# Gated experts with residual: how closing pairs are added up, and the queue of the first weights

## The chip, the cores and the metric

The kernel runs on one core of a Trainium2 chip. The metric is the device time of one execution in microseconds. TensorE (PE) multiplies matrices, VectorE (DVE) and ScalarE (ACT) work element by element and can read and write the PSUM banks that PE fills, GpSimd (POOL) works element by element in SBUF only, and SyncE (SP) issues most transfers. Each engine takes its instructions in the order of its own list, and waits on semaphores for the others.

## The reference

A residual block with 8 gated experts and one shared expert, all in float32, for x of 8 examples, 512 positions and 256 features; F is 1024:

```python
g = einsum('bsd,edf->ebsf', h, Wg)
u = einsum('bsd,edf->ebsf', h, Wu)
expert_outs = einsum('ebsf,efd->ebsd', silu(g) * u, Wd)
expert_output = einsum('be,ebsd->bsd', gating_probs, expert_outs)
shared = einsum('bsf,fd->bsd', silu(h @ Sg) * (h @ Su), Sd)
out = x + (1.0 - sg) * expert_output + sg * shared
```

Every example goes through all experts; the gates (`fside_Bx8_0`, `condB_sharedgateprob`) are 8 numbers and one number for each example.

## The kernel before

**Units.** The batch is cut into two halves of 4 examples, each expert's F into two groups of 4 blocks of 128. One half, expert and group is a unit: 2 x 9 x 2 = 36 units, in that order. In a unit stand 4 weight blocks against 4 examples, 16 products of a block with an example, for Wg, Wu and Wd. The kernel makes them with fewer multiplications than the plain way: for each of the 6 pairs (i, j) in `PAIRS`, products of sums and differences of the operands are shared between (i, j) and (j, i). The numbers `CI` of the four indices give each pair its d = CI[i] - CI[j]; d is 1 for pairs 0, 1 and 4, and 2, 2 and 3 for pairs 2, 3 and 5. GpSimd makes the sums and differences of weights (`make_at`, `w_difference`, `w_sums`, `make_ad`, `d_forms`).

**Two parts.** `gate_up` makes g, u and h of a unit: the hub steps P, Q and R (L466, L489, L511 are matmuls of it, L482 and L484 DVE differences of their results, L472, L499 and L506 ScalarE copies), then for each pair more matmuls (L521), DVE additions (L516, L526), silu on ScalarE (L452) and h on DVE (L457). `h_sums` makes X, the difference of a pair's two h (DVE, L537), and GpSimd adds the h into sums of rows and columns, called rows and cols (`add_sum`, L548).

`down` multiplies by Wd. It keeps running sums in SBUF over all 18 units of a half: accb and accB for each example (the two halves of the 256 features), and accS and accV for each pair. `pair(p)` has three steps: r, a matmul into a bank A (L607), added by DVE into accB (L578); S (or s), whose bank is first filled by a ScalarE copy of accS (L590) before PE multiplies onto it (L591), or s, which starts an empty bank (L607); and a second matmul onto A (L630), which DVE then adds into accV. After pairs come q and p for each example: q (L607) is a matmul on cols, and p (the bank b, L590 and L591) on rows. `put` is what adds a bank into a sum: L578 adds, L580 subtracts, L582 multiplies by a factor and adds.

**Closing.** In the last unit of a half, a pair's V is done and goes into accb of both its examples, +V/d into i and -V/d into j (`closes`). In half 0 all six pairs close in one unit; in half 1, pairs 3, 4 and 5 close one unit earlier, in unit 34, since the last unit makes only pairs 0, 1 and 2 this way. That makes 12 closings, between 1183 and 1231 us, 2349 and 2371 us, and 2393 and 2412 us. A closing is three DVE operations at the end of `pair`: A += accV in the bank (L634), then accb of i and of j from the bank (L578 and L580 where d is 1, L582 twice where it isn't). The two banks that `down` uses, po0 and po1, take turns. A is held (`held`) from the pair's first step to its last, so the other bank serves S; after the closing A's bank is the one that the next product takes (`po_next`).

**Order.** The orders of PE and GpSimd are written out by hand: the strings `HUB`, `BLOCK`, `ORDER`, `FIRST` and `LAST` say when a step of `gate_up` (G) and when one of `down` (D) follows. The down part of a unit starts at G step 22 (`TAKE`) of that unit, and goes on into the next. ScalarE's order is by hand in unit 0 alone. Everywhere else DVE and ScalarE are put in order by a scheduler.

**The start.** `load_gates` issues two transfers on ScalarE's queue, gt (L109) and sgt (L113), of the gates spread over 128 partitions. Everything else comes over SP's queue: the four examples' rows xin (two transfers each, L156) and the four blocks' Wg and Wu (w, two transfers each, L364; 128 partitions x 2 rows of 512 bytes). The first block's Wg stands between the two halves of the first rows, its Wu after them. `first_products` turns the first example and multiplies it with Wg (L202); after it `make_coef` on GpSimd makes the gates' factors (L118 to L121) and `make_at` the sums of the weights (L383 to L387). Transfers use eight semaphores in turn, those of both queues together, and an issue waits until the transfer that used its semaphore before has landed.

Of the kernel before, what the change touches and what calls it, by code (L numbers as in the profile page):

```python
# [11 lines left out]
ALU = mybir.AluOpType  # L12
# [4 lines left out]
def kernel(  # L17
# [37 lines left out]
    nc = tc.nc  # L55
# [24 lines left out]
    hpool = ctx.enter_context(tc.tile_pool(name="h", bufs=11))  # L80
# [16 lines left out]
    gp = nc.gpsimd  # L97
    ve = nc.vector

    def weights(e):  # L100
        return (Wg[e], Wu[e], Wd[e]) if e < E else (Sg, Su, Sd)
# [6 lines left out]
    def load_gates():  # L108
        nc.scalar.dma_start(  # L109
            gt.rearrange("p b e -> p (b e)"),  # L110
            gates.rearrange("b e -> (b e)").partition_broadcast(P),
        )
        nc.scalar.dma_start(sgt, shared_gate.partition_broadcast(P))  # L113
# [20 lines left out]
    def new_po(name, turns=False):  # L134

        k = po_next[0]
        if held[k]:
            k = 1 - k
        if not turns:
            po_next[0] = 1 - k  # L140
        return ps_o.tile([P, S], F32, tag=f"po{k}", name=name), k
# [2 lines left out]
        for t, block in enumerate(blocks):  # L144
            nc.tensor.transpose(bank[:, ts(t, P)], block, ident)

    def load_rows(pool, tag, b, between=None):
        rows = []
        for c in range(2):
            if pool is not iopool:  # L150
                t = pool.tile([P, 2, D], F32, tag=tag, name=f"xin{b}_{c}")
            elif c == 0:
                both = pool.tile([P, NT, D], F32, tag=tag, name=f"xin{b}")
            if pool is iopool:
                t = both[:, 2 * c : 2 * c + 2]
            nc.sync.dma_start(  # L156
                t, x[b].rearrange("(p t) d -> p t d", t=NT)[:, 2 * c : 2 * c + 2, :]
            )
            rows.append(t)
            if between and c == 0:  # L160
                between()
        return rows


# [161 lines left out]
    def touch_banks():  # L326

        banks = [
            pool.tile([P, S], F32, tag=tag, name=f"touch{tag}{k}")
            for pool, tag, n in ((ps_g, "g0", 3), (ps_g, "g1", 3), (ps_o, "po0", 1), (ps_o, "po1", 1))  # L330
            for k in range(n)
        ]
        zero = zpool.tile([P, 2 * S], mybir.dt.bfloat16, tag="z", name="zero")[:, :S]
        ve.memset(zero, 0.0)
        warm = const.tile([P, 1], F32, name="warm")
        nc.scalar.activation(warm, ident[:, 0:1], AF.Silu)
        for bank in banks:
            nc.tensor.matmul(bank, zero[:, 0:P], zero, start=True, stop=True)
# [4 lines left out]
    units = []  # L343
    for h in range(NH):
        for e in range(NE):
            for g in range(GRP):
                u = Unit()
# [8 lines left out]
                u.ad, u.Ud, u.Wd = {}, {}, {}  # L356
                units.append(u)

    def load_w(u, i, ms=(0, 1)):
        if i not in u.raw:  # L360
            u.raw[i] = wpool.tile([P, 2, 2, P], F32, tag="w", name=f"w{u.name}_{i}")
        t = u.raw[i]
        for m in ms:
            nc.sync.dma_start(  # L364
                t[:, m],
                weights(u.e)[m][:, ts(NI * u.g + i, P)].rearrange(
                    "(k p) f -> p k f", p=P
                ),
            )
# [180 lines left out]
    def flush_sums(u, which, n):  # L550
        while any(w == which and k == n for w, k, _ in u.sums):
            add_sum(u)

    def starred(u, p):

        return u.n + 1 < len(units) or p < STARRED

    def closes(u, p):

        return u.closes and starred(u, p) or u.n + 2 == len(units) and p >= STARRED  # L560

    def down(u, acc):

        def tile_of(key):
            acc[key] = apool.tile(
                [P, S], F32, tag=f"acc{key[0]}{key[1]}", name=f"acc{key[0]}{key[1]}_{u.h}"
            )
            return acc[key]

        def put(key, bank, s):  # L570

            if key not in acc:
                if s == 1.0:
                    nc.scalar.copy(tile_of(key), bank)
                else:
                    nc.scalar.mul(tile_of(key), bank, s)
            elif s == 1.0:
                ve.tensor_add(acc[key], bank, acc[key])  # L578
            elif s == -1.0:
                ve.tensor_sub(acc[key], acc[key], bank)  # L580
            else:
                ve.scalar_tensor_tensor(acc[key], bank, s, acc[key], ALU.mult, ALU.add)  # L582

        def seeded(key, w, b):

            po, k = new_po(f"{key[0]}{key[1]}_{u.name}")
            full = key in acc and not turned[k]
            turned[k] = False
            if full:
                nc.scalar.copy(po, acc[key])  # L590
            nc.tensor.matmul(  # L591
                po, w, b, start=not full, stop=True, skip_group_check=full
            )
            return po, full

        def carried(key, w, b):
            po, full = seeded(key, w, b)
            if full:
                nc.scalar.copy(acc[key], po)
            else:  # L600
                put(key, po, 1.0)
            return po if full else acc[key]

        def single(key, w, b):
            po, k = new_po(f"{key[0]}{key[1]}_{u.name}")
            turned[k] = False
            nc.tensor.matmul(po, w, b, start=True, stop=True)  # L607
            return po, k

        def pair(p):  # L610
            i, j = PAIRS[p]
            d = CI[i] - CI[j]
            A, k = single(("r", p), u.Wd[p][i], u.h_[i, j])
            put(("B", j), A, 1.0)
            held[k] = True
            yield
            args = u.Wd[p][j], u.h_[j, i]
            if p in OWN and not closes(u, p):
                carried(("S", p), *args)
            else:  # L620
                if p in OWN:
                    o, full = seeded(("S", p), *args)
                    if not full:
                        ve.tensor_add(o, o, acc["S", p])
                else:
                    o, _ = single(("s", p), *args)
                put(("B", i), o, -1.0)
                put(("V", p), o, -1.0)
            yield
            nc.tensor.matmul(  # L630
                A, u.Ud[p], u.X[p], start=False, stop=True, skip_group_check=True
            )
            if closes(u, p):
                ve.tensor_add(A, A, acc["V", p])  # L634
                put(("b", i), A, 1.0 / d)
                put(("b", j), A, -1.0 / d)
            else:
                put(("V", p), A, 1.0)
            held[k] = False
            po_next[0] = 1 - k  # L640
            yield

        if u.n + 1 < len(units):
            order = (0, 1, 2, 3, 4, "p0", "q0", 5, "q1", "p1", "q2", "p2", "q3", "p3")
        else:
            order = (0, 1, 2, "q1", "q2", "p1", "q0", "p2", "q3", "p0", "p3")
        done = {}
        for what in order:
            if isinstance(what, int):
                yield from pair(what)  # L650
                continue
            i = int(what[1])
            if what[0] == "p":
                flush_sums(u, "rows", i)
                done[what] = carried(("b", i), u.raw_d[:, i, 0:P], u.rows[i])
            else:
                flush_sums(u, "cols", i)
                po, _ = single(("q", i), u.ad[i], u.cols[i])
                put(("B", i), po, 1.0)
                done[what] = po  # L660
            if u.closes and f"p{i}" in done and f"q{i}" in done:
                if CI[i] != 0.0:
                    put(("B", i), done[f"p{i}"], -CI[i])
                for r in (0, 1):
                    ends[u.h, i, r] = acc["bB"[r], i]
            yield
# [67 lines left out]
    def gate_up(u, nxt):  # L734
# [100 lines left out]
    by_hand.enter_context(  # L835
        tc.manual_schedule(engines=HAND | {mybir.EngineType.Activation})
    )
    load_gates()
    touch_banks()
    loaded = []  # L840
    for i in range(NI):
        if i == 0:
            loaded.append(load_rows(hpool, "h", i, lambda: load_w(units[0], 0, (0,))))
            load_w(units[0], i, (1,))
            continue
        loaded.append(load_rows(hpool, "h", i))
        load_w(units[0], i)
    turning = turn_x(0, loaded)
    first_products(units[0], loaded[0])
    for m in range(2):  # L850
# [5 lines left out]
    behind, acc, ahead = iter(()), {}, prepare(1)  # L856
    for u in units:
# [6 lines left out]
        for what in FIRST if u.n == 0 else LAST if nxt is None else ORDER:  # L864
            if what == "G":
                if nG == TAKE:
                    for _ in behind:
                        pass
                    if u.opens:
                        acc = {}  # L870
# [24 lines left out]
            elif what == "X":  # L895
                i, j, pools = TAILS.pop(0)
# [60 lines left out]
```

## Time and profile before

| | |
|---|---|
| three runs | 2445.86, 2445.99, 2448.1 us; median 2445.99 |
| the profiled execution's span, first to last instruction | 2444.9 us |
| lies around the span (median less span) | 1.1 us |
| PE's first and last matmul | 1.19, ends at 2441.08 us |
| DVE: X (L537), two SBUF inputs | 213 times, mean 978 ns |
| DVE: L634 of the closings | 12 times, mean 696 ns |
| GpSimd: sums of rows, further ones (L548) | 282 times, mean 1321 ns |
| GpSimd: sums of columns, further ones (L548) | 282 times, mean 1280 ns |
| GpSimd: first sums of rows and of columns (L548) | 144 times each, means 1385 and 1294 ns |
| median landing of gt and sgt after their issue | 4.0 and 5.7 us |

The profiled execution's own time isn't given apart from its span; the three runs stand for it. A float32 matmul with 512 columns appears as two passes (x2), and its start is 0.43 us after the pass before it where PE isn't kept waiting; so PE is read by the distance of starts, not by the duration of one (593 ns), since passes overlap. In a line of the timeline stand the start and the duration in us, the engine, the line of the kernel, the operation, what it writes and reads, and, in brackets, how long the engine was idle before it and what ended that. A line of the timeline with x2 or more is several instructions in a row. SPq and ACTq are the issues of transfers.

### The profile page before, as it was taken

The numbers are of one execution on the slowest core, as the hardware profiler recorded it, in microseconds if no ns is written. First come the engines' busy times: TensorE is split into PE (matmuls) and PEld (weight loads), VectorE is DVE, ScalarE is ACT, GpSimd is POOL, SyncE is SP. The second block draws the span as 40 slices with busy tenths as digits, with TensorE's granted clock in tenths as the row PEclk, the third lists the DMA queues.
The fourth block names the chain that finished last, engine by engine and source line by source line (L and its number), as shares of the span: only waits on it lengthen the run. The fifth ranks groups of instructions, "written<-read, shape, count | busy, mean of one in ns | idle before, by whom it ended". The sixth has DMA issues, their size and how long they took to land.

```text
span 2444.9 us, 22752 instructions
## 1 busy us (share of the span) xinstructions
PE 2431.5 (99%) x5722; PEld 1079.6 (44%) x5722; DVE 1937.4 (79%) x2889; ACT 1247.2 (51%) x2308; POOL 2095.8 (86%) x2335
## 2 busy tenths in 40 slices
PE   9999999999999999999999999999999999999998
PEld 4444444444444444444444444444444444444444
DVE  7777878777777777787997777777877777777787
ACT  4555554554555555545455555555455455555543
POOL 7988888898988989898888888888888888888883
PEclk9999999999999999999999999999999999999999
DMA  4333333343333333344353222322333333232322
GB/s 160 99 104 112 101 113 114 103 134 100 128 108 97 106 111 95 106 131 126 112 138 119 92 84 90 96 84 88 100 103 103 104 95 95 84 95 89 95 91 82
DMA packets 219793, 255.82 MB, mean 105 GB/s; under 512 B 63632, under 2 KB 156048, under 8 KB 219664
## 3 DMA queue, kind: packets, MB, share of 16 engines
q1 hardware_dynamic: 219376, 254.34, 34.3%
q8 instruction: 48, 0.79, 0.1%
q14 instruction: 81, 0.66, 0.1%
q10 hardware_dynamic: 288, 0.04, 0.0%
HBM read 238.59 MB, written 15.73 MB: 104 GB/s over the span
## 4 chain that ended last, share of the span: by engine, by line
PE 96%; DVE 1%; POOL 1%; DMA 0%; issue 0%; ACT 0%; SPq 0%; DVEq 0%; ACTq 0%; POOLq 0%
PE c L521 30%; PE c L511 15%; PE c L489 10%; PE c L466 10%; PE r L607 7%; PE r L630 7%; PE S L591 5%; PE b L591 5%; PE q L607 5%; PE s L607 2%; PE tail L715 0%; DVE h L457 0%; POOL wd L437 0%; DMA sgt<-ondB_sharedgateprob_dram 0%; DVE accb L582 0%
## 5 line engine op out<-in xcount | busy, mean ns | idle before, releaser
L521 PE MATMUL c<-b,wb 128*128 128x512 f32 x1728 | 847.5, 592 | 0.0
L452 ACT ACTIVATE sg<-c 128x512 f32<-128x512 f32 x576 | 343.8, 597 | 587.2 <-DVE c L526 343.6
L457 DVE SCALAR_TENSOR_TENSOR h<-sg,coef,c 128x512 f32<-128x512 f32 x576 | 427.8, 743 | 235.1 <-PE c L521 132.4
L521 PEld LDWEIGHTS c<-b,wb 128*128 128x128 f32 x1728 | 327.9, 190 | 412.4 <-issue 389.8
L511 PE MATMUL c<-v,u 128*128 128x512 f32 x864 | 441.6, 593 | 1.2 <-ACT c L506 1.2
L548 POOL TENSOR_TENSOR rows<-rows,h 128x512 f32<-128x512 f32 x282 | 372.4, 1321 | 0.0
L548 POOL TENSOR_TENSOR cols<-cols,h 128x512 f32<-128x512 f32 x282 | 361.0, 1280 | 0.0
L516 DVE TENSOR_TENSOR c<-D,c 128x512 f32<-128x512 f32 x432 | 298.9, 692 | 77.8 <-ACT sg L452 57.9
L526 DVE TENSOR_TENSOR c<-c,D 128x512 f32<-128x512 f32 x432 | 298.6, 691 | 18.7 <-PE c L521 18.5
L466 PE MATMUL c<-x,w 128*128 128x512 f32 x572 | 274.5, 592 | 0.0
L404 POOL TENSOR_TENSOR wb<-u,wb 128x256 f32<-128x256 f32 x108 | 79.0, 732 | 222.4 <-ACT wb L402 222.4
L511 PEld LDWEIGHTS c<-v,u 128*128 128x128 f32 x864 | 163.4, 190 | 209.2 <-issue 167.4
L607 PE MATMUL r<-h,wd 128*128 128x512 f32 x426 | 217.5, 592 | 0.0
L630 PE MATMUL r<-X,ud 128*128 128x512 f32 x426 | 217.5, 592 | 0.0
L537 DVE TENSOR_TENSOR X<-h,h 128x512 f32<-128x512 f32 x213 | 208.4, 978 | 6.9
L489 PE MATMUL c<-x,at 128*128 128x512 f32 x432 | 209.6, 593 | 2.4 <-DVE P L482 2.2
L499 ACT COPY D<-c 128x512 f32<-128x512 f32 x284 | 165.9, 584 | 86.8 <-DVE h L457 86.8
L548 POOL TENSOR_TENSOR rows<-h,h 128x512 f32<-128x512 f32 x144 | 199.5, 1385 | 0.0
L548 POOL TENSOR_TENSOR cols<-h,h 128x512 f32<-128x512 f32 x144 | 186.4, 1294 | 0.0
L472 ACT COPY P<-c 128x512 f32<-128x512 f32 x216 | 126.6, 587 | 107.0 <-PE c L466 102.5
L466 PEld LDWEIGHTS c<-x,w 128*128 128x128 f32 x572 | 108.5, 190 | 135.8 <-issue 111.4
L590 ACT COPY S<-accS 128x512 f32<-128x512 f32 x135 | 79.6, 590 | 152.7 <-DVE accV L578 144.9
(110 smaller groups left out, 3478.4 us busy)
## 6 DMA issues: line engine op xcount, KB each, us to landing
b<-xs SPq DMA_DIRECT2D x210, 512.0 KB, 3.6
v<-xs SPq DMA_DIRECT2D x210, 256.0 KB, 2.6
w<-in_L_cond_Wg_dram SPq DMA_DIRECT2D x128, 128.0 KB, 3.4
w<-in_L_cond_Wu_dram SPq DMA_DIRECT2D x128, 128.0 KB, 3.5
wd<-in_L_cond_Wd_dram SPq DMA_DIRECT2D x32, 512.0 KB, 5.0
f<-xd SPq DMA_DIRECT2D x12, 512.0 KB, 3.3
xs<-f SPq DMA_DIRECT2D x18, 256.0 KB, 3.0
xin<-in_x_dram SPq DMA_DIRECT2D x16, 256.0 KB, 4.0
```

What stands on the lines that cost most here:

```text
L452: nc.scalar.activation(s, bank, AF.Silu)
L457: ve.scalar_tensor_tensor(t, u.sg[i, j], coef[:, u.e, b : b + 1], bank, ALU.mult, ALU.mult)
L466: nc.tensor.matmul(bank, u.raw[i][:, m, 0], xhub[u.h, i][:, 0], start=True, stop=True)
L489: nc.tensor.matmul(bank, u.at[i][:, m], xhub[u.h, i][:, 1], start=False, stop=True, skip_group_check=True,)
L511: nc.tensor.matmul(bank, u.U[p][:, m], u.V[p], start=False, stop=True, skip_group_check=True)
L516: ve.tensor_sub(other, u.Ds[j, m], bank)
L521: nc.tensor.matmul(bank, u.W[p][:, r, m], u.VB[p][:, r], start=False, stop=True, skip_group_check=True,)
L526: ve.tensor_add(bank, bank, u.Ds[j, m])
L548: gp.tensor_tensor(sums[n], u.h_[n, n] if first else sums[n], u.h_[at], ALU.add)
L591: nc.tensor.matmul(po, w, b, start=not full, stop=True, skip_group_check=full)
L607: nc.tensor.matmul(po, w, b, start=True, stop=True)
L630: nc.tensor.matmul(A, u.Ud[p], u.X[p], start=False, stop=True, skip_group_check=True)
```

## The change

- In `down`, a closing pair's bank is added into V in SBUF by the one DVE operation that every other pair has too (`put(("V", p), A, 1.0)`), and the bank is let go. The pair is put on a list, `late`.
- `close_late`, called in the first step of the next pair (after its accB addition) or before the next p or q, makes the two results from V: on GpSimd, by two additions in SBUF, where d is 1; on DVE, by `put` with the factor 1/d, where it isn't. So 12 of the 24 results are made by GpSimd (6 in half 0, 6 in half 1).
- The first block's Wg and Wu are issued on ScalarE's queue, ahead of gt and sgt, and no longer among the first rows on SP's. The helper's argument for that (`between`, `ms`) goes.
- PE's order of instructions stays. In the built program DVE has 12 instructions fewer and GpSimd 12 more. In half 0 the two results of pair 5 stand on DVE behind the six operations of the next unit's P steps (L482); the ones before it stand near the place of the closing. SP's issues wait in turn for w0 Wg, w0 Wu, gt and sgt where they waited for gt, the first rows and sgt; block 2's Wu is the one that waits for sgt.

```diff
--- before.py
+++ after.py
@@ -144,7 +144,7 @@
         for t, block in enumerate(blocks):
             nc.tensor.transpose(bank[:, ts(t, P)], block, ident)
 
-    def load_rows(pool, tag, b, between=None):
+    def load_rows(pool, tag, b):
         rows = []
         for c in range(2):
             if pool is not iopool:
@@ -157,8 +157,6 @@
                 t, x[b].rearrange("(p t) d -> p t d", t=NT)[:, 2 * c : 2 * c + 2, :]
             )
             rows.append(t)
-            if between and c == 0:
-                between()
         return rows
 
 
@@ -356,12 +354,12 @@
                 u.ad, u.Ud, u.Wd = {}, {}, {}
                 units.append(u)
 
-    def load_w(u, i, ms=(0, 1)):
+    def load_w(u, i, queue=nc.sync):
         if i not in u.raw:
             u.raw[i] = wpool.tile([P, 2, 2, P], F32, tag="w", name=f"w{u.name}_{i}")
         t = u.raw[i]
-        for m in ms:
-            nc.sync.dma_start(
+        for m in range(2):
+            queue.dma_start(
                 t[:, m],
                 weights(u.e)[m][:, ts(NI * u.g + i, P)].rearrange(
                     "(k p) f -> p k f", p=P
@@ -607,12 +605,27 @@
             nc.tensor.matmul(po, w, b, start=True, stop=True)
             return po, k
 
+        late = []
+
+        def close_late():
+
+            while late:
+                p, i, j, d = late.pop(0)
+                V = acc["V", p]
+                if d == 1.0:
+                    gp.tensor_tensor(acc["b", i], acc["b", i], V, ALU.add)
+                    gp.tensor_tensor(acc["b", j], acc["b", j], V, ALU.subtract)
+                else:
+                    put(("b", i), V, 1.0 / d)
+                    put(("b", j), V, -1.0 / d)
+
         def pair(p):
             i, j = PAIRS[p]
             d = CI[i] - CI[j]
             A, k = single(("r", p), u.Wd[p][i], u.h_[i, j])
             put(("B", j), A, 1.0)
             held[k] = True
+            close_late()
             yield
             args = u.Wd[p][j], u.h_[j, i]
             if p in OWN and not closes(u, p):
@@ -630,12 +643,9 @@
             nc.tensor.matmul(
                 A, u.Ud[p], u.X[p], start=False, stop=True, skip_group_check=True
             )
+            put(("V", p), A, 1.0)
             if closes(u, p):
-                ve.tensor_add(A, A, acc["V", p])
-                put(("b", i), A, 1.0 / d)
-                put(("b", j), A, -1.0 / d)
-            else:
-                put(("V", p), A, 1.0)
+                late.append((p, i, j, d))
             held[k] = False
             po_next[0] = 1 - k
             yield
@@ -649,6 +659,7 @@
             if isinstance(what, int):
                 yield from pair(what)
                 continue
+            close_late()
             i = int(what[1])
             if what[0] == "p":
                 flush_sums(u, "rows", i)
@@ -835,16 +846,14 @@
     by_hand.enter_context(
         tc.manual_schedule(engines=HAND | {mybir.EngineType.Activation})
     )
+    load_w(units[0], 0, nc.scalar)
     load_gates()
     touch_banks()
     loaded = []
     for i in range(NI):
-        if i == 0:
-            loaded.append(load_rows(hpool, "h", i, lambda: load_w(units[0], 0, (0,))))
-            load_w(units[0], i, (1,))
-            continue
         loaded.append(load_rows(hpool, "h", i))
-        load_w(units[0], i)
+        if i:
+            load_w(units[0], i)
     turning = turn_x(0, loaded)
     first_products(units[0], loaded[0])
     for m in range(2):
```

## Prediction

> **What bounds the kernel now.** I read the page first: busy shares, then the chain that ended last.
>
> ```profile
> PE 2431.5 (99%) x5722; PEld 1079.6 (44%) x5722; DVE 1937.4 (79%) x2889; ACT 1247.2 (51%) x2308; POOL 2095.8 (86%) x2335
> ...
> PE 96%; DVE 1%; POOL 1%; DMA 0%; issue 0%; ACT 0%; SPq 0%; DVEq 0%; ACTq 0%; POOLq 0%
> ```
>
> TensorE (PE) is the bound in every stage, so only PE's gaps can be won. PE's order of work isn't changed. The view of PE's waits says which gaps there are (us in total, times, longest):
>
> ```profile
> PE c L489 <- DVE P L482: 2.2, 3, 0.9
> PE S L591 <- ACT S L590: 1.7, 3, 0.6
> PE c L511 <- ACT c L506: 1.2, 1, 1.2
> PE q L607 <- DVE accb L582: 1.1, 1, 1.1
> PE c L202 <- DMA w<-in_L_cond_Wg_dram: 1.1, 1, 1.1
> ```
>
> In the timeline nearly all of them lie in three places: the first 50 us, the closings of half 0 (1183 to 1233) and those of half 1 (2349 to 2412). The first closing, in the timeline:
>
> ```profile
> 1183.77 0.69 DVE L634 TENSOR_TENSOR r<-r,accV 128x512 f32<-128x512 f32 x1
> ...
> 1185.49 0.68 DVE L578 TENSOR_TENSOR accb<-r,accb 128x512 f32<-128x512 f32 x1
> ...
> 1186.10 0.67 DVE L580 TENSOR_TENSOR accb<-accb,r 128x512 f32<-128x512 f32 x1
> ...
> 1186.80 0.59 ACT L590 COPY S<-accS 128x512 f32<-128x512 f32 x1 [1.79 <-DVE accb L580]
> ...
> 1187.44 1.13 PE L591 MATMUL S<-h,wd 128*128 128x512 f32 x2 [0.55 <-ACT S L590]
> ```
>
> Three DVE operations must read the bank before ScalarE may copy S into it, and PE waits for that copy. Each such wait also slows the pass after it by 0.10. Set against PE's usual distance of 0.43 between two passes, the gaps cost: half 0, 0.82 + 0.31 + 0.84 + 0.16 at S and s (L591, L607), plus 1.20 at 1232.87 (L489, behind DVE's queue), together 3.33; unit 34's closings (2371.88, L489) 0.86; the last unit's 0.82 + 0.31 + 1.40 (2396.73, 2404.76, 2412.18) = 2.53. All closings: 6.72 us.
>
> **What the skill says.** The Trainium skill, "SBUF — State Buffer", section "Who interferes with whom", says that a VectorE instruction with two SBUF inputs contends with a GpSimd instruction that reads SBUF, and that the later one is blocked. The trace agrees:
>
> ```profile
> L537 DVE TENSOR_TENSOR X<-h,h 128x512 f32<-128x512 f32 x213 | 208.4, 978 | 6.9
> ```
>
> X (two SBUF inputs) takes 0.69 in its quicker runs and about 1.23 in the others, 0.98 on average; L578, which reads one input from a bank, is always 0.68 to 0.69. GpSimd's hub sums (L548) take 1.27 or, held, 1.72. "DMA: Bandwidth & Descriptors", section "Issuing engines are not separate DMA queues", says that transfers issued by ScalarE and by SP share the same 16 engines and interleave, so the other queue saves issue time only. The trace shows that they run beside each other, not how they share.
>
> **Part 1: closing a pair (12 times).** Before: L634 (0.695) and two results from the bank (0.68 each). After: one addition into V (L578's row on V, 0.685), and the bank is free. So two DVE operations, about 1.2 us of queue, leave the path to PE: the S and s waits go, and so should q L607 at 2412.18. What is late next is ScalarE's copy, which then starts before PE is there. The results come a step later, from V: for pairs 0, 1 and 4 (d = 1) as two GpSimd additions each, for 2, 3 and 5 as two DVE operations with both inputs in SBUF. DVE loses 12 of 2889 instructions.
>
> GpSimd's price: hub sums of this shape follow each other at 1.23 us, so 6 additions in half 0 cost 7.38. Below: they can't cost less than that. Above, every held one costs 0.45 more. The six DVE operations of each half gain a lock: X's mean excess is 0.29 on DVE, and GpSimd's own excess in the trace, 39 us on the hub sums and 18 on the weight differences, over 213 X's, is 0.27 per X. I take 0.27 on GpSimd, from 0 to 0.45.
>
> *Half 0.* PE can be 3.33 earlier, if GpSimd keeps up. GpSimd's idle time there is
>
> ```profile
> 1214.91 0.72 POOL L404 TENSOR_TENSOR wb<-u,w 128x256 f32<-128x256 f32 x1 [1.49 <-PE c L521]
> ...
> 1232.33 1.26 POOL L548 TENSOR_TENSOR cols<-cols,h 128x512 f32<-128x512 f32 x1
> ```
>
> 1.76 (at 1190.37), 2.32 (1198.97) and this 1.49: 5.57; from 1214.91 to 1242 there is none. Four of the DVE operations come before 1232 (pairs 2 and 3): 7.38 + 4 x 0.27 - 5.57 = 2.9 later. The last sum for q of example 2 then ends at 1233.6 + 2.9 = 1236.5. PE's q L607 that needs it ran at 1236.40, and would like to run at 1233.1. So PE waits there for GpSimd instead: -0.1 us in all (+1.0 without the lock; -0.8 with all four held). GpSimd's next idle time, 2.87 at 1244.87, takes the lateness up. ScalarE's b seeds and the DVE operations that now wait for GpSimd's accb (pair 2 waits for pair 1's, done near 1197) have more room. Behind a waiting GpSimd addition stand its hub sums, and PE's p and q behind those.
>
> *Unit 34, pairs 3 to 5.* Two GpSimd additions, 2.46, at about 2362, with no idle time after them until 2383.88 (3.31). The sum for q of example 2 (2371.69 to 2372.96) ends at 2375.4, and PE wanted it at 2374.5 (2375.41 less 0.86): gain 0; with one DVE pair's lock -0.3. I take -0.3 (-0.9 to +0.2).
>
> *Last unit, pairs 0 to 2.* Four GpSimd additions; GpSimd's next products for PE have several us of room here, and the DVE operation that needs accb0 from GpSimd comes 1.3 us after it would be done. I take the whole +2.53 (+1.5 if the lock delays the queue). The wait of b at 2420.55 stays.
>
> **Part 2: the start.**
>
> ```profile
> 0.73 0.41 ACTq L109 DMA_DIRECT2D gt<-in_fside_Bx_dram  x1
> ...
> 6.95 0.20 POOL L118 TENSOR_SCALAR rest<-sgt 128x8 f32<-128x8 f32 x1 [5.64 <-DMA sgt<-ondB_sharedgateprob_dram]
> ...
> 10.20 0.47 SPq L364 DMA_DIRECT2D w<-in_L_cond_Wu_dram  x1
> ...
> 14.99 0.73 POOL L385 TENSOR_TENSOR at<-w 128x256 f32<-128x256 f32 x1 [1.06 <-DMA w<-in_L_cond_Wu_dram]
> ```
>
> The first product's wait (1.36 at 6.88) may shrink by up to 1.0, but that is hidden: GpSimd starts at 14.99 on the fourth weights and is then busy to 39.6, and from there DVE and ScalarE lead to PE's wait of 1.37 at 46.46. What counts is when those weights land: issued 10.20, landed 14.86. SP's issues stand in a row, 0.475 apart, each waiting until an earlier transfer has landed; the row before was let go by sgt's landing at 6.87, seven issues ahead of 10.20. By the built order the same row now waits for w0 Wg, w0 Wu, gt and sgt in turn: w0 Wu seven issues ahead of the last weights, sgt four. Without loss w0 Wu must land by 6.9 and sgt by 8.3. ScalarE's queue then carries 768 small packets where it had 256. In the trace its first 113 went in 1.25 us, near one for one with SP's 141. At 100 in a us, from 2.1: w0 Wg lands near 5.0 and w0 Wu near 7.4, gt and sgt, with SP's first rows through, by 8.5. Then 7.4 + 3.3 = 10.7: 0.5 lost. From +0.5 (faster) to -1.4 (w0 Wg 5.7 after issue, as before). ScalarE's own two extra issues (0.43 each) lie ahead of its first copy at 5.87.
>
> **Sum.** -0.1 - 0.3 + 2.53 - 0.5 = +1.6. The profiled execution's span, 2444.9, becomes 2443.3; the runs' median, 2445.99, is 1.1 above the span, and keeps that: 2444.4.
>
> **Rivals.** *GpSimd doesn't bind* (sums come in time, because idle time elsewhere gives more room): 6.7 gained, 0.5 lost at the start: 2439.8. For it: PE's waits on GpSimd today are nearly nil. Against: the 27 us without idle time in half 0.
> *The lock hurts more:* 0.8, 0.9 and 1.0 less in the three places' low ends: -0.8 - 0.9 + 1.5 - 0.5 = -0.7: 2446.7.
> *ScalarE's queue is slow at the start* (slower than before): gt and sgt, 128 rows each, landed 2.08 apart. At that pace, w0 Wg's 256 rows land at 6.9, w0 Wu's at 11.0, gt at 13.1, sgt at 15.2. Then the fourth weights are issued at 17.1, 6.9 later, and all that follows too: 2445.99 - 2.1 + 6.9 = 2450.8. It decides from the point where sgt lands after 10.4 (a loss over 2.1). For it: it is the only pace on this queue that was measured to its end. Against: that end ran beside SP's largest load.
>
> **Chances.** Forecast 0.46 (its own range 2442.8 to 2445.6), GpSimd free 0.22, lock 0.12, slow queue 0.20. The range is 2440.2 to 2449.5, which leaves out the lower half of the second case and the upper half of the last. 0.2% is 4.9 us, about what a measurement of this kernel can tell from no change. Faster than that (below 2441.1): most of the second case, 0.22 with a little of the first; slower (above 2450.9): half of the last, 0.11; the same 0.67.
>
> **What would show it.** Right: no S wait at 1187, 1204 and 2396; GpSimd without idle time at 1190, 1199 and 1215, and q L607 waiting for cols L548 near 1236 and 2375; accb by DVE from V at 0.7 or 1.2 us; PE's c L511 near 46.5 to 47. Wrong: S still waiting; q not waiting for GpSimd (then near 2440); sgt landing after 10.4 and PE starved of weights before 20 us (then near 2450).

## The result and the profile after

The changed kernel takes 2455.07 us (median of 6 runs, 2453.1 to 2455.54) against 2446.41 for the kernel before (6 runs): a ratio of 1.0033, 95% interval 1.0023 to 1.0044. It is slower by 8.7 us, where 2444.4 was forecast, and the time lies outside the forecast's range. The profiled execution took 2454.76, its span is 2453.0; the 1.8 between them is more than the 1.1 that was taken for before, where the two figures came from different executions.

The busy times from the page of the changed kernel, and then the view of PE's waits in it (lines moved up by two: L519 was L521, L605 was L607):

```profile
PE 2434.2 (99%) x5722; PEld 1079.7 (44%) x5722; DVE 1937.4 (79%) x2877; ACT 1249.2 (51%) x2308; POOL 2113.4 (86%) x2347
```

```profile
PE q L605 <- POOL cols L546: 5.5, 3, 3.3
PE c L509 <- ACT c L504: 2.5, 2, 2.0
PE c L519 <- DMA b<-xs: 2.2, 2, 2.0
PE b L589 <- ACT b L588: 1.3, 2, 1.0
...
PE c L487 <- DVE P L480: 0.7, 1, 0.7
```

The waits of S are gone, those of L487 are down from 2.2 to 0.7, and in their place PE waits for GpSimd's sums, for a load of b and for ScalarE's b. (The 2.0 of L509 lies in the first 50 us.) DVE has 12 instructions fewer and is as busy as before: 1937.4 us in both.

Since PE's order is the same in both kernels, each pass can be set against its own start before. PE is 1.0 us ahead at 1180, 9.0 us behind at 1300 and 7.9 us behind at the end: half 0's closings lose 10.0, unit 34 loses 1.3 (0.86 won, 2.16 lost), the last unit wins 2.4. The place where most is lost, in the timeline of the changed kernel:

```profile
1231.82 2.87 DVE L580 SCALAR_TENSOR_TENSOR accb<-accV,accb 128x512 f32<-128x512 f32 x2
1232.41 1.73 POOL L546 TENSOR_TENSOR rows<-rows,h 128x512 f32<-128x512 f32 x1
1234.10 0.90 POOL L430 TENSOR_TENSOR ud<-ad,wd 128x128 f32<-128x128 f32 x1
...
1235.76 1.72 POOL L546 TENSOR_TENSOR cols<-cols,h 128x512 f32<-128x512 f32 x1
...
1237.53 1.34 PE L605 MATMUL q<-cols,ad 128*128 128x512 f32 x2 [3.28 <-POOL cols L546]
```

Before, the same two results stood here, from the bank:

```profile
1229.77 1.25 DVE L582 SCALAR_TENSOR_TENSOR accb<-r,accb 128x512 f32<-128x512 f32 x2
```

Pair 5's two DVE results take 2.87 where they took 1.25 before, and GpSimd's instructions beside them and beside the addition of xr (L706, also two SBUF inputs) are 0.45 longer each: 1.73 and 1.72 where 1.27 is usual, 0.90 where 0.45 is. The sum that q needs ends at 1237.48, and PE starts then. What follows on PE, in the same view:

```profile
1238.66 1.91 PE L509 MATMUL c<-v,u 128*128 128x512 f32 x2
1240.37 1.70 PE L519 MATMUL c<-b,wb 128*128 128x512 f32 x2
```

In the table of stretches of the changed kernel (length; busy time and count of PE, PEld, DVE, ACT and POOL; then PE's granted clock, the DMA share and GB/s):

```profile
1220.00:1230.00 10.00, 9.71 (x23) 4.10 (x22) 9.41 (x16) 5.70 (x11) 9.84 (x14) 1.00 0.00 0
1230.00:1240.00 10.00, 6.72 (x14) 2.67 (x13) 9.49 (x13) 2.65 (x5) 9.77 (x12) 0.92 0.10 26
1240.00:1250.00 10.00, 9.56 (x21) 3.91 (x20) 6.96 (x12) 5.15 (x10) 6.38 (x10) 0.91 0.22 47
```

After the wait some passes start 0.85 apart instead of 0.43 (called slow passes below), and the granted clock falls to 0.92. That costs 1.8 here and 1.7 once more at 1269, after the next long wait. The Trainium skill, "TensorE: Matmul & The Clock Gate", section "Part 1: The HAM clock gate", says that the array's clock drops to half after an idle window of about 3.4 us and comes back after a busy one. The doubled distance agrees with half the clock; the wait that is enough can be shorter here: slow passes came after waits of 1.9 to 2.6 us too, in 7 of 18 cases (see the end). The next long wait, in the timeline:

```profile
1257.01 0.57 SPq L709 DMA_DIRECT2D out_dram<-xr  x1
1257.76 3.06 SPq L686 DMA_DIRECT2D xr<-in_x_dram  x4
1260.87 2.67 SPq L709 DMA_DIRECT2D out_dram<-xr  x3
1263.64 0.62 SPq L315 DMA_DIRECT2D b<-xs  x1
...
1268.05 1.10 PE L519 MATMUL c<-b,wb 128*128 128x512 f32 x2 [2.03 <-DMA b<-xs]
```

The same transfers before:

```profile
1246.60 3.65 SPq L675 DMA_DIRECT2D xr<-in_x_dram  x4
...
1252.29 2.78 SPq L698 DMA_DIRECT2D out_dram<-xr  x4
1255.17 0.63 SPq L317 DMA_DIRECT2D b<-xs  x1
```

In the built order of before, the reload of xr stands ahead of all four stores of the next example; in the changed kernel one store stands ahead of it, and waits for DVE. The reload, three stores and the load of b follow at SP's pace of 0.7 to 0.9 an issue, and b is issued 8.5 us later than before, while PE was 4.5 behind: the first store comes 4.7 later, the reload behind it makes most of the rest.

The start, in the changed kernel's timeline:

```profile
8.37 0.20 POOL L118 TENSOR_SCALAR rest<-sgt 128x8 f32<-128x8 f32 x1 [7.07 <-DMA sgt<-ondB_sharedgateprob_dram]
...
10.20 0.47 SPq L362 DMA_DIRECT2D w<-in_L_cond_Wu_dram  x1
...
14.70 0.73 POOL L383 TENSOR_TENSOR at<-w 128x256 f32<-128x256 f32 x1 [2.75 <-DMA w<-in_L_cond_Wu_dram]
```

sgt landed 1.4 later than before (8.29 against 6.87), just in time for the fourth weights to be issued at 10.20, as before.

### The profile page after: what moved, and what is told of

It reads as the page before. It is cut to its first block, busy times and chain, and to the rows that moved or that the text cites. A ratio compares the mean times of both kernels' runs of the same rounds, so it can differ in the third digit from the quotient of the medians.

```text
span 2453.0 us, 22752 instructions
## 1 busy us (share of the span) xinstructions
PE 2434.2 (99%) x5722; PEld 1079.7 (44%) x5722; DVE 1937.4 (79%) x2877; ACT 1249.2 (51%) x2308; POOL 2113.4 (86%) x2347
## 4 chain that ended last, share of the span: by engine, by line
PE 93%; POOL 5%; DMA 1%; DVE 1%; issue 0%; ACT 0%; SPq 0%; ACTq 0%; DVEq 0%; POOLq 0%
PE c L519 29%; PE c L509 14%; PE c L464 9%; PE c L487 9%; PE r L605 7%; PE r L643 7%; PE q L605 5%; PE b L589 5%; PE S L589 5%; PE s L605 2%; POOL rows L546 1%; POOL cols L546 1%; DMA b<-xs 0%; POOL wd L435 0%; POOL u L390 0%
## 5 line engine op out<-in xcount | busy, mean ns | idle before, releaser
L519 PE MATMUL c<-b,wb 128*128 128x512 f32 x1728 | 849.2, 593 | 2.2 <-DMA b<-xs 2.2
L519 PEld LDWEIGHTS c<-b,wb 128*128 128x128 f32 x1728 | 328.3, 190 | 416.3 <-issue 392.8
L509 PE MATMUL c<-v,u 128*128 128x512 f32 x864 | 442.8, 594 | 2.9 <-ACT c L504 2.5
L509 PEld LDWEIGHTS c<-v,u 128*128 128x128 f32 x864 | 163.5, 190 | 212.7 <-issue 168.1
L605 PE MATMUL r<-h,wd 128*128 128x512 f32 x426 | 218.4, 594 | 0.0
L487 PE MATMUL c<-x,at 128*128 128x512 f32 x432 | 209.4, 593 | 0.9 <-DVE P L480 0.7
```

The costliest lines, as they stand in the source:

```text
L487: nc.tensor.matmul(bank, u.at[i][:, m], xhub[u.h, i][:, 1], start=False, stop=True, skip_group_check=True,)
L509: nc.tensor.matmul(bank, u.U[p][:, m], u.V[p], start=False, stop=True, skip_group_check=True)
L519: nc.tensor.matmul(bank, u.W[p][:, r, m], u.VB[p][:, r], start=False, stop=True, skip_group_check=True,)
```

## The experiments

The theory after the result (A): the DVE operations with two SBUF inputs and GpSimd hold each other (called the lock below) far longer than was priced, and together with GpSimd's additions make q wait; the rest follows from that. Rivals: GpSimd's additions alone make q wait (B); the start loses the time (C); what is lost after 1238 comes from DVE's late operations and SP's order, whether q waits or not (D), the reload ahead of b above all (E). Each run's time is a median of 5 to 21 runs, the ratio is to the kernel before beside it (2446.5 to 2446.9).

**Which half of the change.** e1_start_only is the kernel before with the second half of the change alone:

```diff
+    load_w(units[0], 0, nc.scalar)
     load_gates()
...
-            loaded.append(load_rows(hpool, "h", i, lambda: load_w(units[0], 0, (0,))))
```

> Only the first weights' queue is changed, closings as before. Theory A (the loss is all in the closings of half 0 and unit 34, the start gains): PE 1.1 us earlier at 70 us, as in the changed kernel, and still so at the end: about 2445.3. Rival C (the new start is what loses, through the transfers that follow it): 2450 or more.

Measured: 2447.01, ratio 1.0000 (0.9992 to 1.0008). PE's lead at 70 us, for which A expected 1.1, was 0.15 in this trace.

e2_closing_only is the changed kernel with the start of before.

> Only the closings are changed, the first weights as before. Theory A: the waits of q for GpSimd near 1237 and 2385 are as in the changed kernel, and the time is that of the changed kernel plus the start's 1.1: about 2456. Rival C: 2446 or less.

Measured: 2453.95, ratio 1.0029 (1.0018 to 1.0040). All waits of the changed kernel from 1215 on are there again. So the closings lose it, and C falls. This run's PE was 0.85 ahead at 70 us with the old start: the first 50 us differ by that much from one execution to the next, and the 1.1 of the changed kernel's trace says little of its start.

**Lock or additions.** e3_no_lock lets pairs 2, 3 and 5 close as before, from the bank (one SBUF input):

```diff
+            if closes(u, p) and d != 1.0:
+                ve.tensor_add(A, A, acc["V", p])
+                put(("b", i), A, 1.0 / d)
+                put(("b", j), A, -1.0 / d)
+            else:
...
```

> As the changed kernel, but pairs 2, 3 and 5 (d not 1) make their results from the bank as before; the GpSimd additions of pairs 0, 1 and 4 stay. Theory A (GpSimd is late because of its six additions and because the DVE operations with two SBUF inputs hold it and are held): lateness 7.4 - 5.6 = 1.8, so q waits at most 1 us near 1237, no slow passes: about 2445 to 2447. Rival B (the additions alone make q wait): q still waits 2 to 3 us near 1237: 2451 to 2454.

Measured: 2446.92, ratio 1.0000 (0.9992 to 1.0008). In its timeline the sum for q of example 2 ends where PE needs it:

```profile
1233.65 1.27 POOL L546 TENSOR_TENSOR cols<-cols,h 128x512 f32<-128x512 f32 x1
...
1235.13 1.02 PE L605 MATMUL q<-cols,ad 128*128 128x512 f32 x2
```

There is no wait in brackets, no slow pass and no wait for b near 1268. All six additions of GpSimd in each half are in: B falls. That e3 is no faster than before has other reasons: of the 1.1 won at S in half 0, 0.7 goes at 1211, where s waits for pair 3's closing, and 0.9 in two short gaps at 1252 and 1260 (0.41 of it idle time that the profile puts down to nothing). The groups by shape show the price, first the changed kernel, then e3:

```profile
L580 DVE SCALAR_TENSOR_TENSOR accb<-accV,accb 128x512 f32<-128x512 f32 x12 | 14.3, 1226 | 0.0
```

```profile
L580 DVE SCALAR_TENSOR_TENSOR accb<-r,accb 128x512 f32<-128x512 f32 x12 | 7.6, 675 | 0.0
```

The same twelve operations take 1226 ns from V in SBUF and 675 from the bank.

e4_no_gpsimd makes all results on DVE, a step late, from V (`put` for every d, no `gp.tensor_tensor`).

> As the changed kernel, but DVE makes the results of pairs 0, 1 and 4 too, a step late from V; GpSimd has no addition more. Theory A: twelve DVE operations in each half compete for the lock, about 1.2 us each in place of 0.68, but GpSimd's own idle time hides its share; q doesn't wait for GpSimd, S waits are gone, some waits for DVE come back: 2442 to 2446. Rival B: as the additions alone did it, all of the closings' gain comes: 2439 to 2441. If q still waits 2 us or more for GpSimd, the lock alone is enough.

Measured: 2457.90, ratio 1.0043 (1.0030 to 1.0055): the slowest of all runs. Its view of PE's waits:

```profile
PE q L605 <- DVE accB L576: 4.1, 2, 2.1
PE c L509 <- POOL wb L402: 4.0, 3, 1.6
...
PE c L519 <- DMA b<-xs: 1.4, 1, 1.4
```

Without any addition on GpSimd, PE loses more. q waits as long as the expectation named, but here for its bank, which a late DVE has to empty. So the lock is enough by itself, on whichever side of it is later. (Here it is twelve such operations in each half, where the changed kernel has six; those six without any addition weren't run.) That is not the 2442 to 2446 which A named: A had still taken DVE's share for hidden.

**Which pair.** e5_pair5_bank is the changed kernel with the condition `p == 5` in place of `d != 1.0` above.

> As the changed kernel, but pair 5 alone makes its two results from the bank, as before. Theory A (the DVE operations with two SBUF inputs and GpSimd hold each other; pair 5's two held GpSimd by 1.4 us right ahead of the sum that q of example 2 needs): q's wait near 1237 falls from 3.3 to about 2, and with it what follows up to 1270 becomes smaller: 2448 to 2452. Rival B (the additions alone): 2454, q waits 3 us or more.

Measured: 2447.26, ratio 1.0003 (0.9994 to 1.0011), 7.8 less than the changed kernel, and less than A expected, for two operations in each half. q near 1238 waits 1.6 instead of 3.3, no slow pass follows, and SP's order is that of before: PE doesn't wait for b.

e6_pair4_later leaves pair 5 and puts GpSimd's additions of pair 4 behind q of example 2. (In half 0, p of example 1 is made before them, and lacks their share: that part is left out.)

```diff
...
-            while late:
-                p, i, j, d = late.pop(0)
+            for what in [k for k in late if k[0] != 4 or at == "p2"]:
+                late.remove(what)
+                p, i, j, d = what
...
```

> As the changed kernel, but GpSimd's two additions of pair 4 stand behind the sum for q of example 2, in half 0 and in unit 34; the DVE operations stay. Theory A: GpSimd's sum comes 2.5 us earlier, q waits about 1 near 1237 and not at all near 2385. If the 7.9 us lost after 1238 follow from that long wait (slower passes, DVE late, stores ahead of the load of b), they are gone: about 2443 to 2446. Rival D (they come from the DVE operations and the order of SP's queue by themselves): the q wait is gone, but PE still waits for b near 1268: 2448 to 2451.

Measured: 2449.47, ratio 1.0012 (1.0003 to 1.0020). The view of PE's waits:

```profile
PE q L605 <- DVE accB L576: 3.2, 2, 1.6
PE c L519 <- DMA b<-xs: 2.5, 2, 1.9
```

q waits 1.6, now for DVE, which empties its bank behind pair 5's two results (2.86 at 1233.49), and no slow pass follows near 1240; but b comes as late as in the changed kernel. So the two parts of what was lost after 1238 have two causes: the slow passes come with the 3.3 us wait, and b's lateness with pair 5's late results and SP's order (D, for that part): e4 and e6, which make these results from V, have a store ahead of the reload too; e5 and e10, which make them from the bank, have before's order.

**SP's order.** e9_no_reload takes away the reload between store and b:

```diff
-                load_back(h, i + 1)
+                back[h, i + 1] = back[h, i]
```

> As the changed kernel, but the rows of x for two examples of half 0 (1 and 3) aren't loaded again: their results are added onto the rows of examples 0 and 2, so the output leaves out that part, and SP's queue has eight issues fewer near 1258 to 1270. Theory E (PE's wait of 2.0 for b at 1268 comes from SP's queue, where in the changed kernel the reload stands behind a store, and b behind both): that wait and the slower passes after it are gone, about 4 us: 2450 to 2452, while q still waits 3.3 near 1237. Rival (b is late because everything on DVE is): b still waits 2 near 1268, 2454 to 2455.

Measured: 2457.57, ratio 1.0041 (1.0027 to 1.0054). The wait for b is gone, as E has it, but nothing is won. In its timeline another wait stands there:

```profile
1264.15 2.36 DVE L706 TENSOR_TENSOR xr<-to,xr 128x512 f32<-128x512 f32 x2
...
1269.07 1.10 PE L509 MATMUL c<-v,u 128*128 128x512 f32 x2 [2.37 <-POOL cols L546]
```

Without the reload the scheduler puts two additions of xr, with two SBUF inputs again, ahead of work that ScalarE waits for: its silu waits 4.8 us for DVE, and its copy of c behind that ends at 1268.97. The profile names GpSimd's sum, which ends at 1269.00, so which of the two PE waited for isn't shown. Two more stretches of slow passes that the changed kernel didn't have (after the waits at 45.8 and 2386.5 us) add to its time. So the reload was what held b, but what b's wait is worth by itself isn't shown.

**What can be kept.** e7_last_unit_only changes the last unit alone (all other closings from the bank), with the new start.

> Closings of half 0 and of unit 34 as before, those of the last unit and the start as in the changed kernel. Theory A: the last unit gains its 2.3 us, the start between 0 and 1: 2443.5 to 2444.5. Rival: the last unit's gain is given back before the end: 2446 or more.

Measured: 2444.91, ratio 0.9992 (0.9984 to 1.0000); 2396.7 to 2412.2 gains 2.5, as forecast, and 0.2 of it goes at 2415.

e8_pairs01_half0 adds pairs 0 and 1 of half 0: `closes(u, p) and u.n + 1 < len(units) and p > 1` goes to the bank.

> As the run with the last unit alone, and pairs 0 and 1 of half 0 changed too (four GpSimd additions, 4.9 us, for which GpSimd had 5.6 us of idle time; no DVE operation with two SBUF inputs). Theory A: another 1.0 us gained at S near 1187 and 1195, q doesn't wait: 2442.5 to 2444. Rival B: additions alone make GpSimd late: q waits near 1236, 2446 or more.

Measured: 2444.51, ratio 0.9988 (0.9982 to 0.9995). S near 1187 and 1195 gains 1.1, and q doesn't wait. In this trace 1.0 goes again in the same two short gaps as in e3; in e12's, with the same closings, they aren't there.

e10_pairs0123_half0 adds pairs 2 and 3 of half 0 (`p > 3` goes to the bank).

> As the run with pairs 0 and 1 of half 0 and the last unit changed, and pairs 2 and 3 of half 0 too (four DVE operations with two SBUF inputs more, no GpSimd addition more). Price of the lock by itself: S near 1204 gains 0.84, then b near 1215 waits about 1.1 for ScalarE behind DVE, as in the changed kernel, and q of example 1 about 0.5; no wait at 1237 over 1 us and none for b at 1268: 2444.5 to 2446. If GpSimd is late enough without pair 4 for q to wait 2 us or more near 1237: 2448 or more.

Measured: 2444.85, ratio 0.9994 (0.9986 to 1.0002). In its trace S wins 0.84, then b at 1215 loses 1.2, and q at 1219 another 1.0, waiting for DVE's accb: four locked operations give back more than the free bank brings. The medians alone don't tell it from e8.

e11_unit34_too is e8 with unit 34 as in the changed kernel.

> As the run with pairs 0 and 1 of half 0 and the last unit changed, and all three pairs of unit 34 as in the changed kernel. Theory A: the 0.66 of L489 near 2372 is won, and q waits 1.9 for GpSimd 3.5 us later: 1.3 slower than that run, 2445.8. Rival: the wait of unit 34 in the changed kernel came from half 0's lateness: 2444.

Measured: 2444.66, ratio 0.9995 (0.9987 to 1.0003). The view of PE's waits has the wait of the changed kernel, though half 0 was in time:

```profile
PE q L605 <- POOL cols L546: 1.9, 1, 1.9
```

Against before, this unit wins 0.86 and loses 2.17, the 1.3 that A names. The median hardly shows it.

e12_old_start is e8 with the first weights on SP's queue as before.

> As the run with pairs 0 and 1 of half 0 and the last unit changed, but with the first weights on SP's queue as before. If the start is worth nothing: 2444.5. If it is worth what the traces showed at 70 us in most runs (1.1): 2445.6.

Measured: 2442.97, ratio 0.9985 (0.9978 to 0.9991), the fastest of all and 3.5 us under the kernel before. The new start isn't worth anything, as e1 said; that e12 is faster than either expectation named even speaks for a small loss by it. Set against the kernel before beside it, each kernel with the new start is slower than the same with the old one: by 0.3 (e1), 1.5 (the changed kernel and e2) and 1.2 (e8 and e12), each time within what the intervals allow. This is the version to keep: pairs 0 and 1 of both halves and pair 2 of the last unit closed from V, the rest from the bank.

## Why the prediction was wrong, step by step

- **A bank freed after one operation removes the S waits:** right. 0.82, 0.31 and 0.83 came in half 0 (forecast 0.82, 0.31, 0.84), and the 2.53 of the last unit in full, of which 0.14 went again at 2415.
- **GpSimd's additions are taken up by its idle time, up to 1.8 us:** right, within 0.3. In e3 the sum for q comes 2.1 later than before, counted from PE's lead at 1180, and q doesn't wait.
- **The price of the lock** is the term of the sum that failed first. It said 0.27 us on GpSimd for each of four operations in half 0, 1.1 together. Counted over all instructions between 1182 and 1242 that are more than 0.1 longer than the quick ones of their shape, GpSimd's excess rose from 3.0 to 5.3 and DVE's from 2.0 to 6.1; each of the six operations has 0.56 of the latter. The sum for q came 4.9 later (2.9 forecast). Three things were wrong:
  - The 0.27 was too low, and the trace of before had the right figure. It came from the hub sums (39) and the weight differences (18) alone, and left out the sums of the weights (`at`). Between 60 and 2440 us of that trace 218 GpSimd instructions are more than 0.1 longer than the quick ones, 101 us in all, 43 of them on `at`. 215 of the 218 overlap in time with a DVE operation with two SBUF inputs; of the other 2049 only 183 do. So such an operation nearly always holds one GpSimd instruction, by 0.45, which the prediction had as its upper end. (X also has more than the two durations named there: 73 of 213 take 0.77 to 1.09. Its mean is right.)
  - Pair 5's two operations were left out because they stand behind six others: that put them right on top of the sum that q needed (e5: 7.8 us for this pair alone). With all six at 0.45 the sum gives 7.38 + 2.7 - 5.57 = 4.5 later. The addition of xr, which came behind that sum before and holds it here, is about the rest.
  - What the lock costs on DVE had no place in the sum.
- **ScalarE's b has more room:** wrong. b at 1215 waits 1.0 behind pair 3's two operations on DVE (2.28); e10 has the same wait without pairs 4 and 5.
- **"GpSimd's next idle time takes the lateness up":** wrong, and the largest miss: the sum put what follows a late q at nothing. Up to q at 1237.53 half 0 had lost 2.1. The other 7.9 came after it: 3.5 in two runs of slow passes, 2.3 at b, 1.2 in short waits for ScalarE; the last 0.9, at 1253 and 1260, stands in e3 and e8 too, and so isn't a sequel of the long wait. The built order of SP's queue, which moved one store ahead of a reload, was there to be read, and the sum didn't look at it.
- **Unit 34:** -0.3 was forecast, -1.3 came, for the same reason: GpSimd's excess there (2349 to 2385) rose from 0.8 to 2.8, against 0.3 in the sum.
- **The start:** its cost of 0.5 wasn't seen in the changed kernel's trace (sgt at 8.3 against "by 8.5", the fourth weights issued at 10.20 as before). It was in e1's: sgt landed at 8.88, and these weights were issued at 10.78. PE's lead at 70 us runs from 1.5 ahead to 0.5 behind in the eleven traces with the new start, and is 0 to 0.9 in the three with the old one; the mean is 0.6 in both. As a median it is nothing within 2 us (e1). The rival of a slow queue, which had sgt at 15.2, falls. The case of a harder lock had the right mechanism, but its ends were set at 0.45 an operation and without anything that follows.

## What to carry to other kernels

Moving a result from a PSUM bank into SBUF frees the bank, but where both inputs of the DVE operation then lie in SBUF, price it at its held duration if GpSimd is busy around it, on both engines, and look at which sum stands beside it. Take that price from every instruction that is held in the trace, not from two kinds of them. A wait that comes to one engine isn't over when that engine goes on: read what queues behind it in the other orders (SP's too), and reckon with slow passes if PE stands still for two or three microseconds. Test such an edit pair by pair: the whole change loses 8.7 us here, and five of its twelve closings kept alone (e12) win 3.5.

## What the runs showed of the hardware

Slow passes of PE (0.85 apart instead of 0.43), over the traces of all 14 kernels here, leaving out the first 40 us: after waits of 3.4 us, counted from the usual distance, they came 3 times of 3; after 1.9 to 2.6 us 7 times of 18; after 0.9 to 1.85 us never in 35. They begin 0.9 to 2.4 us after the restart and are three or four in a row, some 1.3 to 1.8 us lost. What decides in the middle range stays open. A GpSimd instruction that a DVE operation with two SBUF inputs holds is longer by about 0.45, whatever its own length (a hub sum 1.72 for 1.27, a weight form 1.17 for 0.73, a `ud` 0.90 for 0.45), a DVE operation held by GpSimd by 0.2 to 1.1; both can happen around one and the same operation (at 1232 to 1235, DVE 1.19 and 1.76 where 0.68 is usual, GpSimd 1.73 and 0.90), so that a lock can cost twice.
